# Moving one of four first products behind the sums with v in layer 1's attention

## The chip, the cores and the metric

The kernel runs on one NeuronCore of a Trainium2 chip (trn2). The metric is the device time of one execution in microseconds (us). Engines are named as in the profile: PE is TensorE's matmul row and PEld its weight load, DVE is VectorE, ACT is ScalarE, POOL is GpSimd, SP is SyncE.

## The reference, cut to what matters

The whole program is a chain of four layers on x of shape 8 x 512 x 128 (8 batches, 512 tokens, width 128). Each layer is a feed-forward part, a mixer and the same feed-forward part again, with residual sums. The change touches one mixer, layer 1's attention: 16 heads of 8 dimensions, no mask, softmax over all 512 keys.

```python
x = x + pe[:, :S, :]
q = (x @ wq + bq).reshape(B, S, H, Hd).transpose(0, 2, 1, 3)
k = (x @ wk + bk).reshape(B, S, H, Hd).transpose(0, 2, 1, 3)
v = (x @ wv + bv).reshape(B, S, H, Hd).transpose(0, 2, 1, 3)
scores = jnp.einsum('bhqd,bhkd->bhqk', q, k) / math.sqrt(Hd)
attn = jax.nn.softmax(scores, axis=-1)
out = jnp.einsum('bhqk,bhkd->bhqd', attn, v)
out = out.transpose(0, 2, 1, 3).reshape(B, S, D)
out = out @ wo + bo
h = out + x
# then a layer norm over the last axis, times gamma, plus beta
```

Layer 3's attention is the same with a causal mask and runs through the same code with `causal=True`; the change leaves its order as it is.

## The kernel before, in words

The stages run one after the other (`_STAGES`, line 1875), each with its own planning of VectorE, ScalarE and GpSimd. A planner orders these engines' instructions and hands out tile buffers when the program is built; it may put pieces of a later stage among those of an earlier one. In attention's main loop TensorE's order is exempt: `with self.in_order(mybir.EngineType.PE)` (lines 388 and 1496) ties every TensorE instruction to the one emitted before it.

Attention handles one batch after the other; the document calls a batch's share a turn (0 to 7). A softmax needs the row maximum first, and the kernel computes scores twice. The **first products** (`maxima`, lines 1643 to 1689) are q times k, 128 queries by 512 keys, each in a PSUM bank of its own from a pool of three named `first`; VectorE reduces each to a column of negated maxima (line 1673, about 0.6 us each). The 16 heads are stored as four groups g of four heads j, head j of a group on partitions 32j to 32j+31, so a first product uses only 32 of TensorE's 128 rows. When the 16 maxima of one group are there, GpSimd copies them out (line 1679). `maxima_turned` (line 1705) transposes the copies on TensorE for use one turn later.

The **weighted products** (`weighted`, lines 1753 to 1804) compute scores the other way round, keys on partitions. A turn has 16 steps: four groups g times four key chunks c. A step has two halves, one for heads 0 and 1 and one for heads 2 and 3. A half takes a double bank (`pair`, a pool of two), multiplies k and q of two heads into it (line 1770), subtracts the maxima by a second accumulating product with `max_rows` (line 1777), and ScalarE takes the exponential of 128 x 1024 values into `e` (line 1781, about 1.02 us). The second half ends with `product()` (line 1719): the sums with v, four products of the previous step's `e` and v, which land on four column groups of the bank `av` and appear as eight instructions in the trace.

The main loop (lines 1497 to 1504) hands two first products of a later turn to each half, so a step issues four. They come from one iterator over all turns; 64 first products and four more (`lead=4`) are issued before the loop, and the remaining 444 use up the first 222 of the 256 halves. In layer 1 the order of a group and chunk is j = 2, 3, 0, 1 (line 1695): the first half, on heads 0 and 1, gets j = 2 and 3, the second half, on heads 2 and 3, gets j = 0 and 1, so four products on four row groups stand together. Within a half of layer 1 the order on TensorE is: two score products, two first products, two products with `max_rows`; the maxima are reduced after the exponential is emitted (lines 1793 to 1795).

Between halves, `between(b)` (line 1542) places pieces of other turns at fixed slots, a slot being the index of a half (`_SLOTS["l1a"]`, line 229): the end of the turn before (division, transposes, output product, norm: slots 6, 8, 10, 12, 13, 16, 17), the spreading of q and k of the turn after (slots 0 and 12), projections two turns ahead (slots 1 to 16 and 18), and the turned maxima of the next turn at slot 30, the first half of step 15. The pieces with TensorE work all stand at even slots, between the two halves of a step.

Of the kernel before, what the change touches and what calls it, by code (L numbers as in the profile page):

```python
# [291 lines left out]
class _Kernel:  # L292
# [1460 lines left out]
    def weighted(self, b):  # L1753


        nc, sb, causal = self.nc, self.sb, self.causal
        scale = float(1.0 / np.sqrt(np.float32(8)))
        q = self.turns[b]
        q["ctx"] = []
        if b == 0:  # L1760
            self.unmultiplied = None

        def half(g, c, pair, es, firsts):
            q0 = c * P if causal else 0
            n = L - q0
            sc = self.pair()
            heads = (2 * pair, 2 * pair + 1)
            for h in heads:
                r = bass.ts(h, 32)
                self.mm(  # L1770
                    sc[:, h % 2, :n], q["kT"][g][r, bass.ts(c, P)], q["qT"][g][r, q0:], stop=False
                )
            if not causal:
                reads = [first() for first in firsts]
            for h in heads:
                r = bass.ts(h, 32)
                self.mm(sc[:, h % 2, :n], self.max_rows[r, g, :], q["mT"][r, q0:], start=False)
            if causal:
                reads = [first() for first in firsts]
            e = sb.tile([P, 2, L], F32, name="e", bufs=5)  # L1780
            nc.scalar.activation(e[:, :, :n], sc[:, :, :n], AF.Exp, scale=scale)  # L1781
            if causal:
                nc.gpsimd.affine_select(  # L1783
                    e[:, :, :P],
                    e[:, :, :P],
                    pattern=[[0, 2], [1, P]],
                    compare_op=ALU.is_ge,
                    fill=0.0,
                    base=0,
                    channel_multiplier=-1,  # L1790
                )
            es.append(e)
            for read in reads:
                if read:
                    read()
            if pair == 1:
                self.product()
                self.unmultiplied = (q, g, c, es)

        for g in range(4):  # L1800
            for c in range(NC):
                es = []
                for pair in range(2):
                    yield lambda firsts, g=g, c=c, pair=pair, es=es: half(g, c, pair, es, firsts)
# [112 lines left out]
```

## Time and profile before

| what | us |
|---|---|
| median of 3 runs | 2370.53 (2366.5 to 2375.26) |
| span of the profiled execution | 2372.5 |
| that execution's own time | not listed apart from its span |
| layer 1's attention, main loop | about 806 to 1236 |
| PE busy / DVE busy / ACT busy / POOL busy, whole span | 2109.1 / 1631.6 / 1269.6 / 660.6 |
| PE / DVE / ACT busy from 815.74 to 1159.70 (turns 0 to 6, 343.96 us) | 308.53 / 288.30 / 247.26 |
| mean granted TensorE clock, span / 815.74 to 1159.70 / 1167 to 1180 | 0.937 / 0.99 / 0.74 |

A line of the timeline reads: start, duration, engine, line, operation, what is written and read, shapes, number of merged instructions, and in brackets the idle time before it and what ended it. All matmuls carry line 329, that of the helper `mm`, so they are told apart by their tiles: `first<-qkT` are first products, `pair<-qkT` score products, `pair<-mT,max_rows` the products with the maxima, `av<-e,v` the sums with v. A line of the waits reads: who waited, for whom, total us, times, longest us. A line of the chain of waits reads: start, duration, engine, tile or operation.

### The profile page before, as it was taken

How to read it: one execution, taken by the hardware profiler on the slowest of the kernel's cores; microseconds unless marked ns; L12 is line 12 of the kernel's file. 1: busy time of each engine (PE TensorE's matmuls, PEld its weight loads, DVE VectorE, ACT ScalarE, POOL GpSimd, SP SyncE). 2: the span in 40 equal slices, each digit the busy share in tenths (PEclk: the TensorE clock that was granted, in tenths of full speed). 3: DMA queues.
4: the chain of work that ended last, by engine and by line, in shares of the span. 5: the costliest groups of instructions: out<-in, count | busy, mean ns of one | idle time of the engine just before them, and what ended most of it. 6: DMA issues, size and time to landing. Idle time of an engine off the chain costs nothing.

```text
span 2372.5 us, 30011 instructions
## 1 busy us (share of the span) xinstructions
PE 2109.1 (89%) x10967; PEld 1001.9 (42%) x10967; DVE 1631.6 (69%) x3830; ACT 1269.6 (54%) x1857; POOL 660.6 (28%) x923
## 2 busy tenths in 40 slices
PE   7679999979998888999996999896789999999989
PEld 3344444444433333333332444444445444444444
DVE  4556775368888788888827889888776556666611
ACT  3545665323322376777772446666674355555554
POOL 1124433013212011111113233446552123333330
PEclk9778998979999999999997999998897999999999
DMA  3000000000000000000000000000000000000001
GB/s 124 1 1 1 1 1 1 14 10 1 1 1 1 1 1 1 1 1 1 1 1 7 1 1 1 0 1 1 0 1 0 1 1 1 1 1 1 2 1 36
DMA packets 10035, 13.07 MB, mean 6 GB/s; under 512 B 416, under 2 KB 8736, under 8 KB 9760
## 3 DMA queue, kind: packets, MB, share of 16 engines
q1 hardware_dynamic: 7776, 10.11, 1.3%
q8 instruction: 86, 1.41, 0.3%
q10 hardware_dynamic: 2112, 1.05, 0.2%
q14 instruction: 61, 0.50, 0.1%
HBM read 9.06 MB, written 2.10 MB: 5 GB/s over the span
## 4 chain that ended last, share of the span: by engine, by line
PE 60%; DVE 23%; POOL 7%; ACT 7%; issue 3%; DMA 0%; ACTq 0%; DVEq 0%; SPq 0%; POOLq 0%
PE pair L329 11%; PE av L329 8%; PE mm L329 8%; PE po L329 6%; PE pu L329 5%; PE first L329 4%; DVE max L1673 4%; PE pg L329 3%; ACT e L1781 3%; PE ck L329 2%; PE pr L329 2%; DVE act L942 2%; PE big L329 1%; PE ph L329 1%; DVE xn L355 1%
## 5 line engine op out<-in xcount | busy, mean ns | idle before, releaser
L1673 DVE TENSOR_REDUCE max<-first 128x1 f32<-128x512 f32 (+3 forms) x756 | 468.3, 664 | 173.4 <-PE first L329 166.1
L1781 ACT ACTIVATE e<-pair 128x1024 f32<-128x1024 f32 (+3 forms) x512 | 436.5, 864 | 239.3 <-PE pair L329 227.1
L329 PE MATMUL first<-qkT 32*128 32x512 f32 (+3 forms) x896 | 267.9, 443 | 30.5 <-DVE max L1673 28.7
L329 PE MATMUL pair<-qkT 32*128 32x512 f32 (+3 forms) x1024 | 222.5, 454 | 20.0 <-ACT e L1781 14.6
L329 PE MATMUL av<-e,v 128*32 128x512 f32 (+3 forms) x2048 | 238.9, 536 | 0.1
L941 ACT ACTIVATE act<-pg 128x512 f32<-128x512 f32 x144 | 85.6, 596 | 212.9 <-PE po L329 122.0
L329 PEld LDWEIGHTS pair<-qkT 32*128 32x128 f32 x1024 | 95.2, 185 | 233.6 <-ACT e L1781 133.2
L329 PE MATMUL pair<-mT,max_rows 32*128 32x512 f32 (+3 forms) x1024 | 190.4, 374 | 1.7 <-DVE mT L1715 1.7
L329 PE MATMUL pu<-xT,w_moe 128*128 128x512 f32 x288 | 158.4, 632 | 18.8 <-DVE act L942 14.0
L1783 POOL TENSOR_SCALAR_AFFINE_SELECT e<-e 128x256 f32<-128x256 f32 x256 | 103.4, 407 | 253.4 <-ACT e L1781 253.1
L329 PE MATMUL po<-act,w_moe 128*128 128x512 f32 x288 | 161.3, 647 | 5.4 <-DVE act L949 4.2
L329 PE MATMUL pg<-xT,w_moe 128*128 128x512 f32 x288 | 150.5, 620 | 4.4 <-ACT act L941 3.3
L329 PEld LDWEIGHTS first<-qkT 32*128 32x128 f32 x896 | 119.6, 185 | 69.4 <-DVE max L1673 66.9
L942 DVE TENSOR_TENSOR act<-act,pu 128x512 f32<-128x512 f32 x144 | 97.8, 679 | 28.8 <-PE pu L329 23.5
L1679 POOL COPY copies<-max 128x128 f32<-128x128 f32 x64 | 23.6, 424 | 272.4 <-DVE max L1673 272.4
L329 PEld LDWEIGHTS pair<-mT,max_rows 32*128 32x128 f32 x1024 | 96.9, 188 | 3.0 <-DVE mT L1715 2.7
L1673 DVE TENSOR_REDUCE max<-mm 128x1 f32<-128x512 f32 (+3 forms) x108 | 70.9, 665 | 36.7 <-PE mm L329 35.5
L949 DVE TENSOR_TENSOR act<-act,big 128x512 f32<-128x512 f32 x128 | 86.3, 677 | 12.3 <-PE big L329 11.8
L329 PEld LDWEIGHTS pu<-xT,w_moe 128*128 128x128 f32 x288 | 50.2, 196 | 76.8 <-DVE act L942 37.0
L329 PEld LDWEIGHTS po<-act,w_moe 128*128 128x128 f32 x288 | 50.5, 199 | 63.5 <-issue 28.1
L978 POOL TENSOR_TENSOR ge<-ge,w_moe 128x64 f32<-128x64 f32 (+1 forms) x32 | 42.8, 1336 | 119.1 <-DVE ge L976 113.6
L329 PEld LDWEIGHTS pg<-xT,w_moe 128*128 128x128 f32 x288 | 51.1, 195 | 57.2 <-issue 40.1
(423 smaller groups left out, 4398.2 us busy)
## 6 DMA issues: line engine op xcount, KB each, us to landing
w_moe<-in_moe SPq DMA_DIRECT2D x1, 2392.0 KB, 14.0
out<-x SPq DMA_DIRECT2D x8, 256.0 KB, 2.3
x<-in_u ACTq DMA_DIRECT2D x4, 256.0 KB, 6.6
x<-in_u SPq DMA_DIRECT2D x4, 256.0 KB, 6.4
w_mixer<-in_l0a SPq DMA_DIRECT2D x1, 960.5 KB, 8.2
w_mixer<-in_l1a SPq DMA_DIRECT2D x1, 769.0 KB, 4.8
w_ffn<-in_l0f SPq DMA_DIRECT2D x1, 578.0 KB, 7.2
w_ffn<-in_l2f SPq DMA_DIRECT2D x1, 560.0 KB, 3.3
```

What stands on the lines that cost most here:

```text
L329: self.nc.tensor.matmul(out, lhsT, rhs, start=start, stop=stop)
L355: nc.vector.tensor_scalar(xn[:, c, :], x[:, c, :], mv[:, c, 0:1], rstd[:, c : c + 1], ALU.subtract, ALU.mult)
L941: nc.scalar.activation(act, pg, AF.Silu)
L942: nc.vector.tensor_tensor(act, act, pu, ALU.mult)
L949: nc.vector.tensor_tensor(act, act, pw[:, e % 2, :], ALU.mult)
L978: nc.gpsimd.tensor_tensor(ge.rearrange(flat), ge.rearrange(flat), self.wide(before, m), ALU.mult)
L1673: nc.vector.tensor_reduce(mx[:, c, j, gs[0] : gs[-1] + 1], sc, AX.X, ALU.max, negate=True)
L1679: nc.gpsimd.tensor_copy(copies[:, :, :, :, g], mx[:, :, :, g].unsqueeze(3).to_broadcast([P, NC, 4, 8]),)
L1781: nc.scalar.activation(e[:, :, :n], sc[:, :, :n], AF.Exp, scale=scale)
L1783: nc.gpsimd.affine_select(e[:, :, :P], e[:, :, :P], pattern=[[0, 2], [1, P]], compare_op=ALU.is_ge, fill=0.0, base=0, channel_multiplier=-1,)
```

## The change

In the non-causal attention the second half of a step issues only the first of its two first products where it issued both. The other one, fourth of the step, is issued at the end of the half, behind `product()`, and its maximum is reduced right there. The causal attention takes all of `firsts` as before.

```diff
                     sc[:, h % 2, :n], q["kT"][g][r, bass.ts(c, P)], q["qT"][g][r, q0:], stop=False
                 )
+            early = firsts[: 2 - pair] if not causal else firsts
             if not causal:
-                reads = [first() for first in firsts]
+                reads = [first() for first in early]
             for h in heads:
                 r = bass.ts(h, 32)
                 self.mm(sc[:, h % 2, :n], self.max_rows[r, g, :], q["mT"][r, q0:], start=False)
             if causal:
-                reads = [first() for first in firsts]
+                reads = [first() for first in early]
...
             if pair == 1:
                 self.product()
                 self.unmultiplied = (q, g, c, es)
+                for first in firsts[len(reads) :]:
+                    first()()
```

## The prediction

> **What bounds the kernel now.** I read the busy table first (PE 89% of the span, but its ends are modelled), then the waits of layer 1's attention (808 to 1245 us), then the timeline of its steps, then the chain that ended last. The waits name two pairs that hold each other up: VectorE waits for first products, first products wait for VectorE's maxima; and ScalarE's exponentials wait for the score pairs.
>
> ```profile
> PEld pair L329 <- ACT e L1781: 102.9, 142, 1.7
> ACT e L1781 <- PE pair L329: 97.1, 151, 1.9
> DVE max L1673 <- PE first L329: 43.1, 89, 2.8
> PE first L329 <- DVE max L1673: 24.5, 59, 1.7
> ```
>
> In a step (one g and c, two halves) I call the four first products F1 and F2 (first half), F3 and F4 (second half), in order of issue. H are the score products of two heads, M the maxima's products (`max_rows`), AV the sums with v. TensorE keeps the written order: H F1 F2 M, pieces of other turns, H F3 F4 M, AV. Three banks hold first products, so F4 can only start when F1 has been read. There are two kinds of step. One without TensorE pieces, in the timeline:
>
> ```profile
> 1021.24 0.50 PE L329 MATMUL pair<-qkT 32*128 32x512 f32 x2
> 1021.25 0.50 PE L329 MATMUL first<-qkT 32*128 32x512 f32 x2
> ...
> 1021.82 2.48 DVE L1673 TENSOR_REDUCE max<-first 128x1 f32<-128x512 f32 x4 [0.27 <-PE first L329]
> ...
> 1022.56 0.50 PE L329 MATMUL first<-qkT 32*128 32x512 f32 x1 [0.36 <-DVE max L1673]
> ...
> 1023.00 1.07 PE L329 MATMUL av<-e,v 128*32 128x512 f32 x8
> 1023.99 0.50 PE L329 MATMUL pair<-qkT 32*128 32x512 f32 x2
> ...
> 1024.57 2.48 DVE L1673 TENSOR_REDUCE max<-first 128x1 f32<-128x512 f32 x4 [0.27 <-PE first L329]
> ```
>
> It takes 2.75 us and is a loop: F4 at 1022.56, AV 0.44 later, the next H and F1 0.99 after that, VectorE's first maximum 0.58 after that, and 0.75 later (0.69 of maximum, 0.06 of hand-over) the next F4: 2.76. VectorE works 2.48 of it and idles 0.27. The PE wait of 0.36 ahead of F4 is the one that the change goes for. By the timeline 50 steps are of this kind: 8 in turn 0, 7 in each of turns 1 to 6.
>
> Where pieces of other turns stand between the halves, the chain of waits goes another way, through ScalarE:
>
> ```profile
> 920.30 1.00 PE av L329 x8
> 921.30 0.43 PE pair L329
> 921.73 0.20 PE first L329
> 922.07 1.04 ACT e L1781
> 923.15 0.50 PE pair L329 x2
> 923.65 0.23 PE pair L329
> 923.88 1.00 PE av L329 x8
> ```
>
> Here the second H needs a `pair` bank that the first exponential gives back; F4 waits for nobody. Such a step takes 3.57 us and its length hangs on how soon after AV the first H and M run.
>
> **The change, part by part.** Nothing is added or removed: in 111 steps (444 first products are issued in the steps) F4 and its maximum move behind AV. F4 is one matmul of 32x512, no DMA; on TensorE's queue it passes two M and four AV products (eight instructions); on VectorE its maximum stays behind F3's.
>
> *The wait in the 2.75 steps: goes, and comes back as another.* With F4 behind AV the sequence between two AV is F4, H F1 F2 M, H F3 M. Still four first products on three banks, and now the last of them, F3, needs the bank of the first, F4. The loop: F3 to AV 0.44; AV to F4 0.99; F4 to VectorE's start 0.58; F4's maximum and hand-over 0.75; then F3, and M and AV behind it. That is 2.76 again. VectorE has 2.48 of work and the same 0.27 idle. M and the second exponential wait for F3 as they did for F4. Sum over 50 steps: 0.
>
> *Ahead of the next H: a cost.* F4 belongs to head j = 1, partitions 32 to 63, the same as the second H of the next step. The timeline prices two products on the same partitions in succession: M at 1021.58, F3 behind it at 1021.81, 0.23. Products on other partitions start 0.01 apart (1021.24, 1021.25). So the first H runs beside F4, and the second H, then F1, F2 and M, begin 0.23 later. In a 2.75 step the wait ahead of F3 covers that: unhindered it would need some 2.0 (0.57 to F3, 0.44, 0.99), with 0.23 2.24, below 2.75. In a 3.57 step nothing covers it: the first exponential, the second H and AV all shift. I go through the turns: turn 0 has four such steps without another wait (steps 5, 6, 7, 9), turns 1 to 5 six each (0, 3, 4, 5, 7, 9), turn 6 five (0, 3, 4, 5, 6): 39. Left out are step 6, where F2 already waits 0.33 for VectorE, and step 8, whose first H waits 0.61 for an exponential, so F4 slips in before it. In step 7 of turns 1 and 2 F2 waits 1.16 and covers it too: 37 x 0.23 = 8.5 us.
>
> *The rule beside that row.* By the Trainium skill, TensorE: Matmul & The Clock Gate, Part 3 (row/col tiling), matmuls on different row groups start about 4 ns apart and those of one queue stay in order. Were F4 only a fifth tile of the pack, 37 x 0.004 would be 0.1 us and the sum near 1.5; the 0.23 row of this trace, on the same row group, decides.
>
> *The last maximum of a turn: a cost.* In step 15 the copies of the maxima are turned for the next turn, and they wait for the very last maximum of that turn, which is F4 of step 14.
>
> ```profile
> 972.14 2.48 DVE L1673 TENSOR_REDUCE max<-first 128x1 f32<-128x512 f32 x4 [0.27 <-PE first L329]
> ...
> 974.68 0.41 POOL L1679 COPY copies<-max 128x128 f32<-128x128 f32 x1 [10.59 <-DVE max L1673]
> ...
> 975.15 0.66 PE L1711 MATMUL pair<-w_const,copies 128*128 128x128 f32 x4
> ...
> 976.23 0.50 PE L329 MATMUL pair<-qkT 32*128 32x512 f32 x2 [0.42 <-ACT e L1781]
> ```
>
> Step 15 began at 974.32; that maximum ended at 974.62, the copy at 975.09, the transposes began at 975.14. Now F4 starts at 974.32, its maximum runs from 974.90 to 975.59, the copy ends at 976.06 and the transposes start at 976.11, 0.97 later. The second H had 0.42 of wait in hand (until 976.23), so it comes 0.42 to 0.55 later; I take 0.48, which holds the 0.23 of this step. 7 turns x 0.48 = 3.4 us. If VectorE's queue puts the maximum after F1's it is 0.6 more, 4 us over the seven.
>
> *One stall: a gain.* At 893.97 (step 7 of turn 1) F4 waited 1.73 for VectorE, whose queue stood behind a GpSimd sum; AV waited with it, and the next step began at half the clock (M follows H after 0.60 instead of 0.34, and it takes 4.48 instead of 3.57). Behind AV this wait costs about 1.6 less; if the clock does not fall, up to 3.0. I take 2.0.
>
> Sum: 8.5 + 3.4 - 2.0 = 9.9 us slower. It is made against the profiled execution, whose span is 2372.5; no other time of it is shown, and the median of the runs, 2370.53, lies 2.0 below. On that median: 2380.4.
>
> *What no row shows.* Only TensorE's order is written down in this stage. The orders on VectorE, ScalarE and GpSimd, and which bank a tile gets, are a planner's, and it plans anew for the moved F4. From below: a stall such as turn 1's (8.13 against 4.91 in turns 3 to 5) and turn 2's (6.36) disappears, 4.7 us less, and the half clock of 1167 to 1180 (11.65 us for three steps that take 8.25 elsewhere) too, 3.4 less: 8 us. From above: one stall of 3.2 in each turn, 22 us. I take 0, the nearer end, because turns 3 to 5 repeat to within 0.05 us a step.
>
> **Rivals.**
> *The loop breaks, and VectorE is the bound.* If F3 does not have to wait for F4's bank (the planner hands out banks in another turn), the 50 steps fall from 2.75 to the 2.48 that VectorE works: 50 x 0.27 = 13.5 us less, so 9.9 - 13.5, about 4 less than before: 2367. With F4 also hidden beside the H, 2357. For it: VectorE is idle for F products 43.1 us in the stage. Against it: three banks and four products between two AV, in either order. It decides the sign if over 37 of the 50 steps shrink so (37 x 0.27 = 10).
> *F4 costs nothing.* If it starts early enough beside the H, or the waits of the 3.57 steps absorb it, only step 15 and the stall remain: 3.4 - 2.0, 2372. Against it: in the chain of those steps AV, H, F, exponential follow without a gap.
> *The planner makes new stalls.* VectorE's queue is strict: where a norm's piece that waits for GpSimd is put ahead of F4's maximum, F3, M and AV wait too. One 3.2 stall in each turn: 9.9 + 22 = 32 more, 2402; three or four of them, 2391. For it: F4's maximum now comes about 1 us later, so more pieces look ready before it. Against it: no norm piece stands close to F4 in the 2.75 steps.
>
> **How the numbers follow.** Forecast (2.75 steps unchanged, 0.23 in the others): 0.55. New stalls: 0.17. F4 free: 0.16. Loop breaks: 0.12. The likeliest gives 2380. The range takes in the forecast with the planner's lower end (2380.4 - 8 = 2372), F4 free, the loop's nearer half (2364) and the stalls up to five of seven (2380.4 + 16 = 2396): 2364 to 2396. The forecast's own range is 2372 to 2386. A change of 0.5% (11.9 us: below 2358.7 or above 2382.4) is about what a measurement of this kernel can tell from none. Slower than that: the stalls (0.17) and the upper 0.22 of the forecast, 0.39. Faster: half of the broken loop, 0.06. The rest, 0.55, lies within.
>
> **What would show it.** In the changed timeline the 2.75 steps should still be 2.75, with a PE wait of about 0.3 to 0.4 ended by a maximum now ahead of the third product of the step, F3; VectorE idle 0.27 ahead of F4's maximum. The 3.57 steps should read 3.80, with M of the first half 0.57 after F4. In step 15 the transposes should start about 1.8 after the step's F4. I am wrong if the free steps fall towards 2.5 (the loop is broken), if the others stay at 3.57 (F4 is free), or if PE waits of over 1 us for VectorE stand in new places.

## The result and the profile after

| what | before | after |
|---|---|---|
| median, us (12 runs each, side by side) | 2371.12 (2366.5 to 2381.54) | 2381.46 (2373.27 to 2390.62) |
| ratio after / before | | 1.0035 (1.0019 to 1.0051) |
| span of the profiled execution | 2372.5 | 2376.5 (own time 2378.27) |
| from the end of step 2 of turn 0 to the end of step 15 of turn 6 | 378.2 | 390.1 |
| mean granted TensorE clock, span | 0.937 | 0.942 |

The changed kernel is slower, by about 8 us (ratio x 2371: 4.5 to 12.1; the two medians lie 10.3 apart). The two profiled executions differ by 4.0 in span but by 11.9 in layer 1's loop: the rest of the program, whose code is the same, ran 7.9 faster in the second one (from 1240 to 1800 us the granted clock was 0.91 before and 0.93 after). So the places are compared one by one below, and the whole by the runs.

First the waits of layer 1's attention in the changed kernel (who waited, for whom, total us, times, longest).

```profile
PEld first L329 <- DVE max L1673: 119.3, 163, 1.7
ACT e L1782 <- PE pair L329: 116.8, 151, 2.4
...
PE first L329 <- DVE max L1673: 15.7, 54, 1.3
```

The last line is the wait that was moved: 24.5 us in 59 waits before, 15.7 in 54 now. It shrank and did not go. ScalarE's wait for the score pairs grew from 97.1 to 116.8, and that is where the loss shows: every exponential that starts later in a step is idle time of ACT. The first line looks alarming (50.9 before) and is not: F4 is now the first thing behind AV, so its weight load is booked as waiting for a maximum while AV's own products stream; F4 still starts 0.99 after AV.

A step without pieces of other turns (timeline of the changed kernel: start, duration, engine, line, operation):

```profile
1026.97 0.49 PE L329 MATMUL first<-qkT 32*128 32x512 f32 x1
...
1027.50 2.48 DVE L1673 TENSOR_REDUCE max<-first 128x1 f32<-128x512 f32 x4 [0.22 <-PE first L329]
...
1028.25 0.50 PE L329 MATMUL first<-qkT 32*128 32x512 f32 x1 [0.19 <-DVE max L1673]
...
1028.69 1.06 PE L329 MATMUL av<-e,v 128*32 128x512 f32 x8
...
1029.68 0.49 PE L329 MATMUL first<-qkT 32*128 32x512 f32 x1
```

Read it as the predicted loop: F3 at 1028.25, AV 0.44 later, F4 0.99 after that, VectorE's maximum of F4 0.53 after F4, and 0.75 later the next F3 (1030.96): 2.71, where 2.75 stood before. The wait is there again, 0.19 ahead of F3, and VectorE idles 0.22 ahead of F4's maximum instead of 0.27 ahead of F1's.

A step with pieces of other turns (step 3 of turn 3, the same view):

```profile
991.15 0.50 PE L329 MATMUL first<-qkT 32*128 32x512 f32 x1
...
991.15 0.50 PE L329 MATMUL pair<-qkT 32*128 32x512 f32 x1
...
991.49 0.39 PE L329 MATMUL pair<-qkT 32*128 32x512 f32 x1
...
992.20 1.02 ACT L1782 ACTIVATE e<-pair 128x1024 f32<-128x1024 f32 x1 [0.76 <-PE pair L329]
...
993.27 0.50 PE L329 MATMUL pair<-qkT 32*128 32x512 f32 x2 [0.15 <-ACT e L1782]
```

F4 and the first H start together; the second H, on F4's rows, only comes 0.34 later, the second M, on the same rows again, comes later still, and the exponential starts 1.05 after the step's beginning (0.83 before, in the same step: 986.96 to 987.79). The H of the second half wait for that exponential, so the whole step takes 3.79 instead of 3.57.

The loss by place, after minus before, summed over the turns; a step's length is counted from the first instruction behind AV to the next such instruction:

| steps | predicted | measured |
|---|---|---|
| free steps (49; the 50th is where the stretch begins) | 0 | -2.2 (2.75 to 2.71) |
| 0, 3, 4, 9 | 24 x 0.23 = 5.5 | 5.8 (0.27, 0.22, 0.31 and, in turns 0 to 5, 0.22 each; step 9 of turn 6 gained 0.34) |
| 5 and 6 | 9 x 0.23 = 2.1 | 3.2 (step 5: 4.26 to 4.73 in turns 1 to 5) |
| 7 and 8 | 4 x 0.23 - 2.0 = -1.1 | 2.1 (turn 1: 1.5) |
| 15 | 3.4 | 3.0 (3.57 to 4.00) |
| sum | 9.9 | 11.9 |

### The profile page after: what moved, and what is told of

Its sections match the earlier page's. It is cut to its first block, busy times and chain, and to the rows that moved or that the text cites. A ratio compares the mean times of both kernels' runs of the same rounds, so it can differ in the third digit from the quotient of the medians.

```text
span 2376.5 us, 29951 instructions
## 1 busy us (share of the span) xinstructions
PE 2111.9 (89%) x10907; PEld 1005.8 (42%) x10967; DVE 1632.2 (69%) x3830; ACT 1265.0 (53%) x1857; POOL 662.4 (28%) x923
## 3 DMA queue, kind: packets, MB, share of 16 engines
q8 instruction: 86, 1.41, 0.3%
q10 hardware_dynamic: 2112, 1.05, 0.2%
## 4 chain that ended last, share of the span: by engine, by line
PE 58%; DVE 23%; POOL 8%; ACT 7%; issue 4%; DMA 0%; ACTq 0%; DVEq 0%; SPq 0%; POOLq 0%
PE pair L329 9%; PE av L329 8%; PE mm L329 8%; PE first L329 6%; PE po L329 6%; PE pu L329 5%; DVE max L1673 4%; PE pg L329 3%; ACT e L1782 3%; PE ck L329 2%; DVE act L942 2%; PE pr L329 2%; PE big L329 1%; PE ph L329 1%; DVE xn L355 1%
## 5 line engine op out<-in xcount | busy, mean ns | idle before, releaser
L1782 ACT ACTIVATE e<-pair 128x1024 f32<-128x1024 f32 (+3 forms) x512 | 431.1, 864 | 255.1 <-PE pair L329 248.0
L329 PE MATMUL first<-qkT 32*128 32x512 f32 (+3 forms) x896 | 273.1, 449 | 22.1 <-DVE max L1673 19.9
L329 PE MATMUL pair<-qkT 32*128 32x512 f32 (+3 forms) x1024 | 245.1, 444 | 18.1 <-ACT e L1782 9.4
L329 PE MATMUL pair<-mT,max_rows 32*128 32x512 f32 (+3 forms) x1024 | 209.5, 382 | 1.6 <-DVE mT L1715 1.6
L329 PEld LDWEIGHTS pair<-qkT 32*128 32x128 f32 x1024 | 109.2, 186 | 136.7 <-ACT e L1782 76.6
L329 PEld LDWEIGHTS pair<-mT,max_rows 32*128 32x128 f32 x1024 | 102.7, 188 | 4.0 <-DVE mT L1715 2.7
```

What stands on the lines that cost most here:

```text
L329: self.nc.tensor.matmul(out, lhsT, rhs, start=start, stop=stop)
```

## The experiments

**1. Is the loop of the free steps closed by F4's bank?** If F4's maximum is what F3 waits for, a shorter maximum of F4 shortens every free step, and a shorter one of F1 does nothing; in the kernel before it is F1's that counts. Three kernels leave out half of one maximum (it reads 256 of 512 keys).

```diff
+                part = sc[:, :, : L // 2] if not causal and j == 1 else sc
                 nc.vector.tensor_reduce(
-                    mx[:, c, j, gs[0] : gs[-1] + 1], sc, AX.X, ALU.max, negate=True
+                    mx[:, c, j, gs[0] : gs[-1] + 1], part, AX.X, ALU.max, negate=True
```

j == 1 is F4; the second kernel has j == 2 (F1), the third has j == 2 in the kernel before.

> The changed kernel, but the maximum of F4 (head 1 of each group, everywhere in layer 1) reads only 256 of its 512 keys, so half of that maximum is left out. Theory (the loop of a free step now runs from F4 over its maximum to F3's bank, then AV, then F4): F4's maximum falls from 0.69 to about 0.42 and the free steps (slots 20 to 27) from 2.71 to about 2.44. Rival, VectorE's total work is the bound: it falls by 0.27 as well, but so it would with any maximum shortened; only the pair with the next kernel tells. Rival, TensorE's own order is the bound: stays 2.71.

> The changed kernel, but the maximum of F1 (head 2 of each group) reads only 256 of its 512 keys, half of that maximum left out. Theory of the loop through F4: free steps stay at 2.71, VectorE's idle time in a step grows from 0.23 by 0.27 to about 0.5. Rival, VectorE's work is the bound: free steps fall by 0.27 to 2.44, as with F4's maximum shortened. Rival, the wait of before still runs through F1: also about 2.44.

> The kernel before, but the maximum of F1 reads only 256 of its 512 keys, half of that maximum left out. Theory: before the change the loop runs over F1's maximum to F4's bank, so here the free steps fall from 2.75 to about 2.48, where the same cut in the changed kernel gains nothing. Rival, VectorE's work is the bound in neither: 2.75 stays.

One run each, beside 2370.59 of the kernel before. F4 short in the changed kernel: 2345.9, free steps 2.44 instead of 2.71. F1 short in the changed kernel: 2371.91, free steps still 2.71. F1 short in the kernel before: 2349.57, free steps 2.48 instead of 2.75. Changed kernel with a short F1:

```profile
1017.29 2.22 DVE L1674 TENSOR_REDUCE max<-first 128x1 f32<-128x512 f32 x4 [0.48 <-PE first L329]
...
1018.04 0.49 PE L329 MATMUL first<-qkT 32*128 32x512 f32 x1 [0.32 <-DVE max L1674]
```

VectorE has 0.26 less to do and waits 0.26 longer; F3 still starts 0.75 after F4's maximum began. So VectorE's total does not bound these steps, before or after. What does is one maximum on a ring: the first product behind AV in the new order, F1 in the old. Step 5 reads 4.49 in both changed kernels (4.73 without the edit): there either maximum counts, which is taken up below.

**2. Two products behind AV.** If the ring is what holds, a second product behind AV should lengthen it.

```diff
-            early = firsts[: 2 - pair] if not causal else firsts
+            early = firsts[: 2 - 2 * pair] if not causal else firsts
```

> Both first products of the second half (F3 and F4) are issued behind AV, each with its maximum. Theory: the last first product ahead of AV is then F2 of the first half, which waits for F3's bank; from there to AV stand M, H, M (about 0.9 to 1.0 where 0.43 was), so the free steps grow from 2.71 to about 3.2 and the 3.57 steps stay near 3.80 (both heads' rows taken, still one product's time): some 25 us over before, ratio about 1.010. Rival, the wait goes as soon as enough is moved behind AV: free steps towards 2.5, ratio below 1.003. Rival, each moved product costs its own time: ratio about 1.007, free steps near 2.75.

Measured: 2527.16 (4 runs), ratio 1.0649 (1.0596 to 1.0703), far more than expected. At full clock the free steps are as expected, 3.15 to 3.17: F2 waits for F3's bank, and both M stand behind it. A step with pieces of other turns (step 9 of turn 2, from 1012.20) and a free one (step 14 of turn 2, from 1029.50):

```profile
1013.48 0.50 PE L329 MATMUL first<-qkT 32*128 32x512 f32 x1 [0.55 <-DVE max L1673]
...
1030.78 0.49 PE L329 MATMUL first<-qkT 32*128 32x512 f32 x1 [0.54 <-DVE max L1673]
```

The steps of the first kind are a miss, at full clock too: 3.80 was expected, and steps 3, 4 and 9 read 4.64 to 4.66 wherever the clock is full, about 1.08 more than before. F2 waits there until 1.28 after the step's beginning, and the first exponential, behind both M, starts 1.92 after it instead of 0.83. The expectation had the wait for F3's bank in the free steps alone. The clock adds to this. The table by windows of the same kernel (window, length, busy time and count of PE, PEld, DVE, ACT and POOL, granted clock, share of the DMA engines, GB/s):

```profile
1104.00:1129.00 25.00, 23.22 (x104) 7.65 (x100) 12.43 (x20) 9.69 (x10) 0.41 (x1) 0.50 0.00 1
```

From 1104 to 1129 the clock is at 0.50; a free step takes 5.01 there and AV 1.94 instead of 1.07. So the wait was met and the size was not: the expectation left the wait out of the steps with pieces of other turns, and it priced all steps at full clock.

**3. Is the 0.23 the price of equal rows?** The order of the heads is turned so that the product behind AV is j = 3 (partitions 96 to 127), on which the next H does not stand.

```diff
-            return [(c, j, (g,), 0) for g in range(4) for c in range(NC) for j in (2, 3, 0, 1)]
+            return [(c, j, (g,), 0) for g in range(4) for c in range(NC) for j in (2, 0, 1, 3)]
...
-            early = firsts[: 2 - pair] if not causal else firsts
+            early = firsts[: 1 + pair] if not causal else firsts
```

The main loop gives one product to a first half and three to a second, so that j = 2 stands in the first and j = 0, 1 and 3 in the second.

> As the change, one first product of each step behind AV, but it is the one of head 3, whose 32 rows no product of the next first half uses (the first half then issues head 2 alone, the second half heads 0 and 1). Theory (the 3.80 steps pay 0.23 because F4 sits on the rows of the second H): they fall to 3.57, the free steps stay at 2.71, the first step after the turned maxima stays at 4.00 (it waits for the last maximum's copy, not for rows), and the step with the output product keeps the 0.24 by which three maxima stand ahead of VectorE's sum: about 4.50. Ratio to before 1.001. Rival (the place behind AV costs, on whatever rows; or VectorE's later maximum does): the steps stay at 3.80, ratio 1.0035.

Measured: 2372.29 (12 runs), ratio 1.0010 (0.9993 to 1.0027). Step 3 of turn 3, which took 3.79:

```profile
986.07 0.49 PE L329 MATMUL first<-qkT 32*128 32x512 f32 x1
...
986.07 0.50 PE L329 MATMUL pair<-qkT 32*128 32x512 f32 x2
...
986.90 1.02 ACT L1783 ACTIVATE e<-pair 128x1024 f32<-128x1024 f32 x1 [0.61 <-PE pair L329]
```

Both H start with the product behind AV, M follows after 0.34, the exponential after 0.83, and the step takes 3.57. Steps 3, 4 and 9 read 3.57 to 3.60, the free ones 2.71. So the place behind AV alone does not cost the 0.23. This kernel also has one product fewer in the first half, where F2 could wait for a bank. A step of the changed kernel in which no bank is late tells the two apart, step 9 of turn 4 (F4; F1 and F2; the second H; both M):

```profile
1074.97 0.50 PE L329 MATMUL first<-qkT 32*128 32x512 f32 x1
...
1074.98 0.52 PE L329 MATMUL first<-qkT 32*128 32x512 f32 x2
1075.31 0.40 PE L329 MATMUL pair<-qkT 32*128 32x512 f32 x1
1075.31 0.62 PE L329 MATMUL pair<-mT,max_rows 32*128 32x512 f32 x2
```

F1 and F2 start within 0.03 of F4. The first M starts 0.34 after F4, as before; the second H also starts 0.34 after it, and the second M (merged with the first in the last line) 0.58. The exponential follows at 1.06 and the step takes 3.80. Only the products on F4's rows are late, and the 0.23 is, to 0.01, what the second M loses: it started with the first M before. Step 15 (3.99) stays, since its cause is the late maximum; step 0 (3.84) stays too, since VectorE holds it, as is shown further down. The miss: step 5 was expected at 4.50 and read 4.26. With this order two maxima, not three, stand ahead of VectorE's sum, which is the second sign for what is found below. Steps 7 and 8 of turns 3 to 5, of which the expectation says nothing, lose 0.92 together against the kernel before (0.39 in the changed kernel): F2 waits for a bank until 1.16 after the beginning of step 7. The Trainium skill, TensorE: Matmul & The Clock Gate, Part 3 (row/col tiling), says that products on different row groups run side by side; here the trace agrees: at 986.07 three products on three row groups start within 0.01, while two on one row group stand 0.34 apart behind AV in the changed kernel.

**4. Each kind of step alone.** `LATE` names the steps whose F4 goes behind AV; that F4 is then the first product of the next step.

```diff
+        LATE = (0, 1, 9, 10, 11, 12, 13)
...
-            early = firsts[: 2 - pair] if not causal else firsts
+            early = firsts[: 2 - pair] if not causal and 4 * g + c in LATE else firsts
```

The second kernel has LATE = (2, 3, 4, 5, 6, 7, 8, 15). F4 of step 14 stays in place in both.

> F4 behind AV only where the next step is free of other turns' pieces (steps 0, 1, 9 to 13), elsewhere as before. Plain bookkeeping (cost only where a busy step follows): all 0.23 go, the gain of 0.04 stays, ratio 0.999. Theory of the loop (three banks, what counts is how many first products stand between two AV): steps 2 and 14 then have five between two AV, so F4 waits for F1's maximum behind F4's of the step before, about 1.92 after the step's start, and these steps take 3.3 instead of 2.71; steps 1 and 10 to 13 2.71, busy steps 3.57: ratio 1.002 to 1.003.

> The other part alone: F4 behind AV in steps 2 to 8 and 15, elsewhere as before. Theory: the busy steps 0, 3 to 9 pay as in the changed kernel (3.80 and more), step 15 does not (3.57, its last maximum is early), and step 2, which has only three first products between two AV, no longer waits and falls from 2.75 to about 2.2: ratio 1.003 to 1.004. Rival without the loop: step 2 stays at 2.75, ratio 1.005.

Only free steps: 2371.57 (12 runs), ratio 1.0016 (0.9998 to 1.0033). Steps 1 and 10 to 13 read 2.71, and the steps with pieces of other turns stand as before (step 15 at 3.57); but steps 2 and 14, which get the late F4 of the step before and keep their own, have five products between two AV and read 3.30:

```profile
1033.52 1.09 PE L329 MATMUL first<-qkT 32*128 32x512 f32 x2 [0.19 <-DVE max L1673]
```

The fourth and the fifth each wait for a bank, one maximum apart, and AV comes 2.30 after the step's start instead of 1.71. Only busy steps: 2377.3 (10 runs), ratio 1.0027 (1.0012 to 1.0043): steps 3, 4 and 9 at 3.80 to 3.95, step 5 at 4.73, step 15 at 3.57, the free ones 2.75, and step 2, with three products left between two AV, 1.94 (2.2 expected). So the loss lies in the busy steps and in step 15. And a free step is worth 1.94, 2.71 or 3.30 for three, four or five products on three banks.

**5. A use of that.** If the fourth product costs a free step 0.5 and more, and a busy step can take a fifth beside its other work, products should be moved from the one kind to the other. From the kernel before, a plan gives each step's number of products in the first half beyond two, and in the second half; in the second half those beyond two stand between M and AV. The order of the heads follows the plan, and in the first three kernels five products, not four, are issued ahead of the loop.

```diff
+                        extra, second = _PLAN[at // 2]
+                        n = 2 if causal else (2 + extra, second)[at % 2]
+                        maxima = [next(self.all_maxima, None) for _ in range(n)]
...
-                reads = [first() for first in firsts]
+                reads = [first() for first in firsts[:2]]
...
+            reads = [first() for first in firsts] if causal else reads + [first() for first in firsts[2:]]
```

First: three in seven free steps, five in seven busy ones, with the fifth in the first half (between M and the pieces of other turns).

> From the kernel before: all first products ahead of AV again, but not four in every step. Free steps issue three (one in the second half), seven of the nine busy steps five (a third one behind M of the first half, where TensorE waits for an exponential), the other two four; five instead of four ahead of the loop. Theory: with three products between two AV on three banks nothing waits for a bank, so the 49 free steps fall from 2.75 to about 2.2 to 2.3, 22 to 27 us; the busy steps give some back where VectorE has a division or a norm besides five maxima (steps 3, 7, 8, 15: up to 0.5 each, 14 us): ratio 0.990 to 0.997. Rival (VectorE's work per turn is the bound, 49 of 57 us): ratio about 1.000 or above, the busy steps growing by what the free ones lose.

Measured: 2367.2 (10 runs), ratio 0.9989 (0.9974 to 1.0004), a miss. The free steps fell to 2.10 and 2.38 as expected, but steps 0 (4.01), 3 (4.27), 7 (5.31; 4.91 before) and 8 (4.29) grew: the rival. Next the fifth in the second half, in six busy steps, and the same with step 0 and one free step left at four.

> As the kernel with three and five, but the fifth product of a busy step is issued in the second half behind M, directly ahead of AV, and only where VectorE has room by its rows: steps 0, 4, 5, 7, 9 and 15; steps 3, 6, 8 and 14 keep four, the other free steps (1, 2, 10 to 13) three. Theory: the free steps with three stay at 2.10 and 2.38 (about 0.5 less than before, 6 in a turn, 21 us in all), a fifth product there waits for no bank and costs at most 0.1, so some 15 to 20 us under before: ratio 0.992 to 0.995. Rival (VectorE's work per turn is the bound): the steps 0, 4, 5, 7 grow by 0.3 to 0.6 each and the ratio stays at 0.998 to 1.000.

> The same with step 0 at four products as well (its VectorE also writes the turned maxima), so step 2 has four: five free steps with three. Theory: step 2 is 2.75 again, 0.4 to 0.5 more in a turn than the kernel beside it, unless step 0 pays that much there: ratio 0.993 to 0.996. Rival as there.

Measured: 2375.38, ratio 1.0019 (1.0003 to 1.0035), and 2373.88, ratio 1.0014 (0.9998 to 1.0029), 12 runs each. Both miss. Steps 6 and 7 went to 5.9 (5.33 and 4.92 before) and step 8 to 4.4 to 5.9. Step 0 reads 4.17 in both, with five products and with four, so its own fifth is not the cause. In the first of the two, step 6 of turn 3:

```profile
998.09 1.87 DVE L1676 TENSOR_REDUCE max<-first 128x1 f32<-128x512 f32 x3
...
998.82 1.09 PE L330 MATMUL first<-qkT 32*128 32x512 f32 x2 [0.31 <-DVE max L1676]
```

All three products of step 5's second half have their maxima read in step 6, behind VectorE's sum and a norm's piece that waited for GpSimd, so F1 and F2 wait for banks and M comes 1.41 after the H instead of 0.82. Steps 5 and 7 have no room on VectorE, whatever room TensorE has. So the fifth product went only where VectorE has room: steps 0, 4 and 9 (three free steps at three); then 0, 4, 8 and 9 (free steps 1, 2, 10 and 11 at three).

> The fifth product only in steps 0, 4 and 9, away from the norm and the division, and step 15 at four again; steps 1, 10 and 11 have three, all others four. Theory (what was lost in the two kernels before is VectorE's queue ahead of steps 0 and 6 to 8): steps 0, 6, 7, 8 are back at 3.57, 5.33, 4.91, 3.57; three free steps a turn at 1.95 to 2.3 instead of 2.75, 1.4 a turn, 10 us: ratio 0.995 to 0.997. Rival (VectorE's work per turn is the bound): 0.999 or above.

> The same and a fifth product in step 8 too, so that step 2 has three: four free steps shorter, 1.9 a turn, 13 us, if step 9 takes the 0.28 by which VectorE's work in step 8 (five maxima, 3.1, and 0.75) is over 3.57: ratio 0.994 to 0.997. Rival as there.

Measured: 2363.94 (12 runs), ratio 0.9973 (0.9958 to 0.9988), and 2357.19 (6 runs), ratio 0.9938 (0.9916 to 0.9961): faster than both kernels; the first lies just outside its forecast of 0.995 to 0.997. Steps 0 and 6 to 8 of the first are back (3.58, 5.31, 4.92 and 3.57) but for turn 1, where steps 8 and 9 take 6.28 and 5.05. Two free steps of the last one, with three products and then four:

```profile
1011.08 0.50 PE L330 MATMUL pair<-qkT 32*128 32x512 f32 x2
...
1013.34 0.50 PE L330 MATMUL pair<-qkT 32*128 32x512 f32 x2
...
1014.65 0.49 PE L330 MATMUL first<-qkT 32*128 32x512 f32 x1 [0.25 <-DVE max L1676]
```

Without a fourth product no product waits for a bank and the step takes 2.26; with it 2.75. Steps 8 and 9 pay 0.18 and 0.24 for their fifth, steps 0 (3.58) and 4 (3.59) next to nothing.

## Why the prediction was right, and where it was not

**The forecast held:** 2380 against a median of 2381.46 (9.9 us slower, where the ratio gives 8.3 and layer 1's loop 11.9), and the mechanism that was named is in the main the one that the runs show. By its own steps:

**The wait comes back (right).** The loop F3, AV, F4, maximum, F3 was forecast at 2.76 and is 2.71. Halving F4's maximum takes 0.27 off it, halving F1's nothing: the ring hangs on F4's bank. The term was 0 and is -2.2 us: F4, alone at the head of the queue behind AV, reaches VectorE after 0.53 where 0.58 had been taken from F1's row. 0.04 to 0.05 in each of 49 steps makes the 2.2.

**0.23 in the busy steps (right).** 5.5 was forecast for steps 0, 3, 4 and 9, and 5.8 came; turning the rows takes it away in steps 3, 4 and 9. The way there differs in one point: the prediction let "the second H, then F1, F2 and M" begin 0.23 later, as in a queue that keeps its order. In step 9 shown above F1 and F2 start 0.01 to 0.03 after F4, 0.3 ahead of the second H that is written in front of them, and the first M is on time; only the second H and the second M are late. So these starts do not bear out the order within a queue that the prediction cites. The price comes out the same because the exponential needs both M. Step 4 pays 0.08 more, since F2 there waits for a bank until 0.55 after the step's beginning. Step 0 (0.27) has another cause than the one given, though with nearly the same price. Step 0 of turn 3 in the changed kernel (from 981.88):

```profile
980.95 0.75 DVE L1715 SCALAR_TENSOR_TENSOR mT<-pair,w_heads,m_lead 128x512 fp32r<-128x512 f32 x1 [0.64 <-ACT m_lead L1713]
...
981.62 2.68 DVE L1673 TENSOR_REDUCE max<-first 128x1 f32<-128x512 f32 x4
...
982.36 0.49 PE L329 MATMUL first<-qkT 32*128 32x512 f32 x1
```

The late transposes of step 15 make `mT` late, and F3's maximum of step 15 stands behind it (from 981.62). F2 needs that bank and starts at 982.36, 0.48 after the step's beginning, with M behind it. The kernel with other rows shows the same 0.47 (977.28 after 976.81), and so its step 0 gained nothing. Where only the busy steps have the late product, `mT` is early, and step 0 reads 3.79: there it is the rows.

**Step 5 (mis-sized).** It lost 0.47, not 0.23. VectorE's row was not followed there. Step 5 of turn 3 in the changed kernel:

```profile
999.37 1.89 DVE L1673 TENSOR_REDUCE max<-first 128x1 f32<-128x512 f32 x3 [0.92 <-PE first L329]
...
1001.17 0.68 DVE L1845 TENSOR_TENSOR o<-pair,w_mixer 128x512 f32<-128x512 f32 x1
...
1001.91 0.50 PE L329 MATMUL pair<-qkT 32*128 32x512 f32 x2 [0.27 <-DVE o L1845]
```

The sum `o` of the norm to come stands behind three maxima (F4, F1, F2) where it had two (F1, F2) ahead of it: it starts 2.33 after the step's beginning instead of 1.86. The second H needs the bank that this sum gives back, waits 0.27 for it and starts at 3.07 instead of 2.60. Halving F4's or F1's maximum gives 0.24 back (4.49), and the other order of heads, with two of them ahead of `o`, all of it (4.26).

**Step 15 (right).** Transposes forecast about 1.8 after the step's beginning, measured 1.75; the term 0.48 is 0.43:

```profile
979.18 0.41 POOL L1679 COPY copies<-max 128x128 f32<-128x128 f32 x1 [10.42 <-DVE max L1673]
...
979.64 0.66 PE L1711 MATMUL pair<-w_const,copies 128*128 128x128 f32 x4 [0.80 <-POOL copies L1679]
```

GpSimd's copy starts when the first of the three maxima, F4's, is through (978.42 plus 0.7), the transposes wait 0.80 for it, and the second H comes 2.34 after the step's beginning instead of 1.91. In the kernels that leave F4 of step 14 in place the step stays at 3.57.

**The stall of turn 1 (wrong).** The sum took 2.0 off for it; steps 7 and 8 of turn 1 lost 1.5 more instead (12.6 to 14.1). In the changed kernel:

```profile
892.73 0.29 DVE L339 BATCH_NORM_STATS2 xn_st<-x 128x6 f32<-128x128 f32 x1 [2.90 <-POOL x L1857]
...
894.06 0.50 PE L329 MATMUL first<-qkT 32*128 32x512 f32 x1 [1.33 <-DVE max L1673]
```

VectorE stands behind the same GpSimd sum as before. The wait only changed its owner: F3 has it now, ahead of the same AV, 1.33 where F4 had 1.73. In step 8 F4's maximum then stands behind the norm's pieces and F2 waits another 0.43, and VectorE's next projection (`trail`) starts at 896.57 where it started at 895.49. The half clock was not avoided either: over 892 to 907 the granted clock is 0.89 in both kernels, but it falls later, on the second half of step 8 (AV at 900.47 takes 1.92), where before it lay on AV of step 7 and the first half of step 8. The step that failed is "behind AV this wait costs about 1.6 less": the ring that had just been written down for the free steps says that F3 inherits the wait of F4, and it was not applied here.

**The rivals.** The loop does not break (experiments 1 and 4). F4 is not free (3.57 to 3.79 in step 3). New stalls were small: turns 3 to 5 lose 0.39 each in steps 7 and 8, of which 0.16 was not forecast. In step 7 F2 waits for a bank until 0.62 to 0.65 after the step's beginning, and the H of the second half come 0.4 later, not 0.23. Step 8 is as forecast: F4 starts while the first H waits for an exponential, 0.68 ahead of it, so that a step counted from F4 on only looks shorter in step 7 (by 0.30) and longer in step 8 (by 0.68). Turn 6 gained 1.15 in its steps 7 to 9, 1167.97 to 1179.62 before and 1179.13 to 1189.63 after; the granted clock over them is 0.71 before and 0.84 after. That is part of the 3.4 that the prediction had named as a possible gain; why the half clock was shorter is open. The two errors, -2.2 in the free steps and +4.2 in the other terms, offset each other in part, so that the total is nearer than the terms are: that much of the nearness is luck.

## What to carry to other kernels

Between two passes that take the whole array, count the products against the banks: with more products than banks, some product waits for the reading of an earlier one, and moving one past the pass only names another waiter; what helps is to take the surplus product to a stretch where both the array and its reader have room. In these runs a product that is put ahead of others delays, apart from the bank that it takes, only those on the same rows, so choose its rows. A wait that comes to stand in the first half of a step with other work costs there as well: two products behind AV cost 0.41 in a free step and 1.08 in such a step. And follow the reader of a moved result in its own queue: one maximum more ahead of an unrelated sum cost as much again as the moved product itself.

## What was not expected of the hardware

The clock held at half over tens of us in the kernel with two products behind AV, although PE was busy 23.22 of 25.00 us there: 0.50 from 1104 to 1129, with steps of 5.01 that repeat. Matmul durations follow it (AV 1.94 against 1.07), so it is no artefact of the clock row. In the kernel before, with PE busy 21.97 of 24.00 us from 1036 to 1060, it was 1.00. The number of matmuls does not tell the two apart: 104 in 25 us against 167 in 24, but the slow clock itself makes the steps long, and from 1000 to 1030 the same kernel ran 174 in 30 us at 1.00. The Trainium skill, TensorE: Matmul & The Clock Gate, Part 1 (the HAM clock gate), says that some 3.4 us of sustained activity release the full clock. This trace does not agree, unless the short waits (0.36 ahead of F2 in each step) keep that activity from counting as sustained. Against that, the kernel before has a wait of 0.36 in each free step too and kept 1.00; no run here tells what decides, and it stays open.
